# Routing statistics on ScalarE, scatters ahead of weight fetches, and layer 1's first scores ahead of the last tile's projections, in a two-layer AdaLN kernel

## The chip, the cores and the metric

The kernel runs on one core of a Trainium2 chip, as one program that computes both layers. The metric is the device time of one execution in microseconds (us). All arithmetic is in float32. Engines are named as in the profile: PE (TensorE, matrix products and transposes), PEld (its weight loads), DVE (VectorE), ACT (ScalarE), POOL (GpSimd, which also issues the indirect DMAs) and SP (SyncE, which here only issues DMAs). Each engine works through its own instructions in a fixed order.

## The reference

Eight sequences of 512 tokens, 256 values a token. Each layer is an attention part and an expert part; each part normalises the token, scales and shifts it by values made from a conditioning vector, and adds its result times a gate to the token. Layer 0's attention is a recurrence with a 16 x 16 state per head; its experts are chosen by argmax, one of eight for each token. Layer 1's attention is causal softmax attention with a table of relative biases; its experts are all computed and mixed by thresholded softmax weights.

```python
# layer 0, attention: q, k, v = silu(x @ W); q, k of unit length; beta = sigmoid(x @ Wbeta)
def step(M, inp):
    q_t, k_t, v_t, b_t = inp
    out_t = jnp.einsum('bnh,bnhd->bnd', q_t, M)
    retrieved = jnp.einsum('bnhd,bnd->bnh', M, k_t)
    delta = v_t - retrieved
    M = M + b_t[..., None, None] * jnp.einsum('bnh,bnd->bnhd', k_t, delta)
    return (M, out_t)
...
# layer 0, experts: one of 8 per token
top_idx = jnp.argmax(gate_logits, axis=-1)
for e in range(8):
    h = relu(x @ w1[e] + b1[e]);  out = out + (top_idx == e) * (h @ w2[e] + b2[e])
...
# layer 1, experts: weights below 0.1 are dropped, the rest are scaled to sum 1
for e in range(8):
    out = out + weights[:, e:e + 1] * (x @ expert_w[e] + expert_b[e])
```

## The kernel before

**Tiles.** A tile is 128 positions of each of the eight sequences; there are four (`NT`), `i` counts them and `b` the sequences. Numbers from L1 on are lines of this kernel.

**Layer 0** runs one `scan` per tile: 128 steps of the recurrence, each four DVE instructions (L741 multiply, L745 reduce, L751 multiply, L756 subtract). The side work of the scan is a list of *pieces*, each with a place, which is a scan step. `run` puts a piece into the program when the scan reaches its place, and it may not be scheduled ahead of that step's instruction; apart from that the order on each engine is the scheduler's. During the scan of tile i there are three kinds of side work:

- `front(i+1)`: statistics, normalisation and projections of the next tile's tokens. Its sums are made on ACT (L498 the sum, L504 the squares, L509 the root); DVE takes the root's reciprocal at L525.
- `follow(i-1)`: what comes after the recurrence for the tile before. `attend` makes the tokens' outputs (root mean square by ACT L919, DVE L934) and adds them to the tokens, then its `stats` take mean and variance of the outgoing tokens for the routing (DVE L950, L951, then the root on ACT, L126, and DVE L132). `route` normalises (L1013), transposes (L1018), makes the gate's logits (L1036, L1051), finds the expert and then a *slot* number for every token (L1114): tokens are sorted by expert into 15 slots of 128 rows. `experts` writes the tokens to their slots in DRAM by eight indirect DMAs (`scatter`, L1130), and works through the slots: `turn` loads a slot's rows (SP issues it) and transposes them (L1169, L1173), `fetch` gets the slot's weights by an indirect DMA of POOL (L1149, two parts, two buffers each), the slot's first half is the first product (L1192) and its activation (L1201), its second half the second product (L1211), whose result goes back to DRAM (L1216 to L1218).
- gathers of finished results and their addition to the tokens in DRAM (L1265, L1266).

Pieces of `experts` are steps of one generator, taken by `on`. The first slots of a tile are done in the same scan (places from 70), slots `late` to 14 in the next scan's list `rest`. Slots 12 to 14 of tile 2 are worked during `follow(3)`, which has no scan beside it and runs after scan 3. A piece `behind("ranks")` may not be scheduled ahead of the routing's last product on PE (L1083), `behind("attention")` not ahead of the attention part's end.

**Layer 1** starts with `prologue`, which normalises (L120 to L183) and projects (L240, L257) the tokens of sequence 0, for tiles 0 to 2 and then for tile 3, whose tokens arrive last. Then a loop over steps `n`: `scores` (L1433 PE, L1442 DVE adds the bias and takes the least, L1447 ACT's exponential), `turn` (L1459 transposes, copied by L1466 and L1468), `weigh` (L1480), and for the sequence before, `tail`, with the expert part: `weights_T` (L1590 transposes the mixing weights, L1592 copies them) and `experts` (L1598 multiplies them with the eight bias rows, L1600 copies that out, L1604 the experts' products, L1609 their weighted sum). All PSUM tiles come from `bank()`, which goes around the 7 banks of layer 0 and the 8 of layer 1.

Of the kernel before, what the change touches and what calls it, by code (L numbers as in the profile page):

```python
# [19 lines left out]
P = 128  # L20
# [43 lines left out]
def tile_two_layers(ctx: ExitStack, tc: tile.TileContext, t: dict, out: bass.AP):  # L64
# [157 lines left out]
    def prologue(b, got, xs, parts=(tuple(range(NT)),)):  # L222
# [13 lines left out]
        def values(i):  # L236
# [7 lines left out]
            w1["ready"] = nc.vector.tensor_add(  # L244
# [3 lines left out]
            ).ins  # L248
# [29 lines left out]
    with ExitStack() as l0:  # L278
# [485 lines left out]
        def attend(i, qk, V, x1, norms):  # L764
# [180 lines left out]
            def stats(b):  # L945
                h = b // 4
                if b % 4 == 0:
                    got["mv", h] = fp.tile([P, 4, 2], F32, tag="mvf", name=f"mvf{i}_{h}")
                st = fp.tile([P, 6], F32, tag="stf", name=f"stf{i}_{b}", bufs=4)
                nc.vector.bn_stats(st, x1[b])  # L950
                nc.vector.bn_aggr(got["mv", h][:, b % 4, :], st)  # L951
                if b % 4 == 3:
                    norms.append((got["mv", h], deviation(fp, "f", got["mv", h])))
# [12 lines left out]
            for h in range(2):  # L966
                pieces.append((16 * h + 25, lambda h=h: roots(h)))
                for b in range(4 * h, 4 * h + 4):
                    pieces.append((13 * h + 25 + b, lambda b=b: rest(b)))
                    pieces.append((12 * h + 30 + b, lambda b=b: stats(b)))  # L970
            return got, pieces

        def route(i, h, norms):
# [31 lines left out]
            for half in range(2):  # L1005
                rs, off = scale_offset(fp, "f", *norms[half])
# [76 lines left out]
            issued["ranks"] = nc.tensor.matmul(  # L1083
# [3 lines left out]
            ).ins  # L1087
# [51 lines left out]
        def experts(i, slot, idx, scatter):  # L1139
# [37 lines left out]
            for j, part in ((0, 0), (0, 1), (1, 0)):  # L1177
                fetch(j, part)
            with tc.issue_after(issued["fetch"]):
                scatter()  # L1180
            yield
            turn(0)
            for j in range(NSLOT):
# [21 lines left out]
                fetch(j + 1, 1)  # L1205
                yield
# [12 lines left out]
                fetch(j + 2, 0)  # L1219
# [16 lines left out]
            if i == NT - 1:  # L1236
                rows = [w1["rows"][:, b * D : (b + 1) * D] for b in range(B)]
                for b in range(B):
                    gather(b, rows[b])
                nc.vector.tensor_mul(rows[0], rows[0], gates[1][:, 0, :])  # L1240
                nc.vector.tensor_add(w1["xs"][:, i, :], rows[0], x_last)
                yield
                with tc.issue_after(w1["ready"]):
                    for b in range(1, B):
                        nc.vector.tensor_mul(rows[b], rows[b], gates[1][:, b, :])
                        nc.gpsimd.dma_start(x2d[b][i], rows[b], accum_op=ALU.add)
# [22 lines left out]
        def follow(i, qk, V):  # L1269
# [20 lines left out]
            def behind(what):  # L1290
                with tc.issue_after(issued[what]):
                    on()

            pieces += [(34, begin), (42, more), (51, more), (57, more), (60, more), (62, settle)]
# [4 lines left out]
                NT - 1: (0, 4, [10 * j for j in range(NSLOT)]),  # L1299
                NT - 2: (12, 4.3, [43, 61, 61.4]),  # L1300
            }.get(i, (11, 4.6, [8, 22, 40, 61]))
            rest = []
            for j in range(NSLOT):
                for half in range(2):
# [3 lines left out]
                    place = starts[j - late]  # L1308
                    if i == NT - 1:
                        rest.append((place + 3 * half, on))  # L1310
                    elif place < 43:
                        rest.append((place + 3 * half, on))
                    else:
                        what = "ranks" if place > 60 else "attention"
                        rest.append((place + 0.2 * half, lambda what=what: behind(what)))
# [8 lines left out]
        def load1():  # L1324
# [16 lines left out]
            put("eb", [NE, D], t["expert_b"])  # L1341
# [67 lines left out]
        for k, piece in enumerate(begun):  # L1409
            place = 102 + 4 * k if k < NT + 2 else 145 + k if k < NT + 4 else 201 + k  # L1410
            last.append((place, piece))
# [6 lines left out]
    with ExitStack() as l1:  # L1418
# [3 lines left out]
        gw, gbias, eb, ew = (w1[key] for key in ("gw", "gbias", "eb", "ew"))  # L1422

        def scores(b, c, i):
# [12 lines left out]
            for r in range(4):  # L1437
# [4 lines left out]
                nc.vector.tensor_tensor_reduce(  # L1442
# [6 lines left out]
            return made.ins  # L1449
# [40 lines left out]
        def tail(b, got):  # L1490
# [6 lines left out]
            wt = lp.tile([P, NT, NE], F32, tag="wtd", name=f"wtd{b}")  # L1497

            ys, yTt, stats, wTs = {}, {}, {}, []
# [62 lines left out]
            def weights():  # L1562
# [14 lines left out]
                nc.vector.scalar_tensor_tensor(  # L1577
# [197 lines left out]
```

## Time and profile before

| | us |
|---|---|
| median of 3 runs | 2201.99 (2200.83 to 2203.8) |
| the profiled execution | 2209.05 |
| its span | 2207.3 |
| scan 0, 1, 2, 3 (first L741 to last L756) | 244.8, 259.1, 264.4, 249.5 |
| last scan's end to the slot numbers of tile 3 | 1077 to 1166 |
| experts of tile 3, first to last product | 1199 to 1336 |
| layer 1, first scores to the end | 1353 to 2207 |

The span is the part of the execution that the profile covers; the rest of the profiled execution's time lies around it. Busy time over the whole span: PE 1730.0, DVE 1582.4, ACT 1080.0, POOL 640.6 us. In a row of a timeline the bracket at the end gives how long the engine had been idle before the instruction and what ended that.

### The profile page before, as it was taken

To read this page: it belongs to the slowest core of one execution; us is meant where nothing else is said; L and a number is where in the kernel's file an instruction comes from. 1 tells how busy PE (TensorE), PEld (TensorE's weight loads), DVE (VectorE), ACT (ScalarE), POOL (GpSimd) and SP (SyncE) were. 2 spreads that over 40 slices of the span, in tenths; PEclk is the share of its full clock that TensorE was granted. 3 is DMA by queue.
4 is the path that set the end of the run, shared out by engine and by line. 5 is a ranking of instruction groups with operands and counts; after the bars stand their busy time and mean duration, and the time that the engine had idled before them with its cause. 6 is when DMAs were issued, how large, how long until landed. Compare 5 with 4: busy or idle time off the path is not lost. (4 is left out here: it accounts for less than half of the span.)

```text
span 2207.3 us, 32493 instructions
## 1 busy us (share of the span) xinstructions
PE 1730.0 (78%) x10906; PEld 1208.3 (55%) x10906; DVE 1582.4 (72%) x4523; ACT 1080.0 (49%) x2674; POOL 640.6 (29%) x920
## 2 busy tenths in 40 slices
PE   5342047479885898649886798999999999999988
PEld 4221035269673786549765785555555555555544
DVE  5999999979989799899751004677676666666654
ACT  5253035554466545414341236785657474756421
POOL 1313013355353554524463643011110101010210
PEclk8676577689887999869997998999999999999998
DMA  5110000358104580139863873000101000010101
GB/s 165 49 50 5 0 1 11 103 181 321 50 18 138 188 325 36 49 119 335 190 124 138 288 236 71 1 20 11 27 11 25 13 22 15 20 20 6 23 17 12
DMA packets 88630, 189.58 MB, mean 86 GB/s; under 512 B 13688, under 2 KB 67104, under 8 KB 75664
## 3 DMA queue, kind: packets, MB, share of 16 engines
q0 software_dynamic: 33696, 137.43, 19.5%
q1 hardware_dynamic: 54768, 50.09, 7.9%
q8 instruction: 86, 1.41, 0.3%
q14 instruction: 80, 0.66, 0.1%
HBM read 175.10 MB, written 36.93 MB: 96 GB/s over the span
## 5 line engine op out<-in xcount | busy, mean ns | idle before, releaser
L1447 ACT ACTIVATE pr<-sc,low 128x384 f32<-128x384 f32 (+3 forms) x512 | 255.7, 556 | 197.2 <-DVE low L1442 193.8
L1442 DVE CUSTOM_DVE_ANT_0 sc<-ps,strips 128x384 f32<-128x384 f32 (+3 forms) x512 | 225.8, 486 | 87.1 <-PE ps L1433 56.3
L1192 PE MATMUL ps<-hTs,w 128*128 128x128 f32 x1920 | 243.8, 289 | 12.6 <-DMA w<-in_wrows,idx 7.8
L1192 PEld LDWEIGHTS ps<-hTs,w 128*128 128x128 f32 x1920 | 239.4, 204 | 19.9 <-issue 10.9
L745 DVE TENSOR_REDUCE state<-terms 128x16 f32<-128x272 f32 x512 | 227.3, 444 | 15.5
L1211 PE MATMUL ps<-w,act 128*128 128x256 f32 x960 | 226.4, 391 | 11.5 <-DMA w<-in_wrows,idx 8.9
L756 DVE TENSOR_TENSOR state<-state,upd 128x256 f32<-128x256 f32 x511 | 222.7, 436 | 15.0
L1604 PE MATMUL ps<-ew,hTd 128*128 128x512 f32 x512 | 232.6, 608 | 0.0
L741 DVE TENSOR_TENSOR terms<-state,K 128x256 f32<-128x256 f32 x512 | 216.2, 422 | 14.8
L751 DVE TENSOR_TENSOR upd<-K,state 128x256 f32<-128x256 f32 x511 | 214.4, 420 | 16.0
L1201 ACT ACTIVATE act<-ps,w 128x128 f32<-128x128 f32 x480 | 136.6, 372 | 148.2 <-PE ps L1192 139.5
L1211 PEld LDWEIGHTS ps<-w,act 128*128 128x128 f32 x960 | 183.8, 197 | 37.9 <-issue 7.6
L1459 PE MATMUL ps<-cst,pr 128*128 128x128 f32 x1280 | 191.7, 295 | 14.5 <-DVE low L1442 11.6
L1609 DVE SCALAR_TENSOR_TENSOR accd<-ps,wtd,accd 128x256 f32<-128x256 f32 x256 | 123.8, 483 | 100.9 <-PE ps L1604 86.4
L1459 PEld LDWEIGHTS ps<-cst,pr 128*128 128x128 f32 x1280 | 149.6, 149 | 83.6 <-DVE low L1442 24.0
L1613 POOL TENSOR_TENSOR accd<-accd,bc_g 128x256 f32<-128x256 f32 x28 | 20.3, 726 | 547.0 <-DVE accd L1609 547.0
L1149 POOL DMA_INDIRECT w<-in_wrows,idx x120 | 124.3, 1036 | 186.8 <-ACT hTs L1173 78.3
L1604 PEld LDWEIGHTS ps<-ew,hTd 128*128 128x128 f32 x512 | 96.4, 193 | 120.4 <-issue 106.6
L1433 PE MATMUL ps<-kT,qTc 32*128 32x128 f32 (+3 forms) x1024 | 132.3, 491 | 4.4 <-DVE low L1442 2.7
L1468 DVE COPY prT<-ps 128x512 f32<-128x512 f32 (+3 forms) x256 | 117.1, 484 | 10.3 <-PE ps L1459 10.0
L1466 ACT COPY prT<-ps 128x512 f32<-128x512 f32 (+3 forms) x256 | 98.6, 413 | 7.9 <-PE ps L1459 7.5
L1480 PE MATMUL ps<-prT,v 128*32 128x512 f32 (+3 forms) x1024 | 96.6, 448 | 0.0
(296 smaller groups left out, 2890.7 us busy)
## 6 DMA issues: line engine op xcount, KB each, us to landing
hs<-zero SPq DMA_DIRECT2D x4, 1920.0 KB
hslot<-hs SPq DMA_DIRECT2D x60, 128.0 KB
ys<-ysb POOLq DMA_DIRECT2D x60, 128.0 KB
x<-in_x SPq DMA_DIRECT2D x32, 128.0 KB
strips<-strip_d SPq DMA_DIRECT2D x16, 256.0 KB
out<-accd POOLq DMA_DIRECT2D x32, 128.0 KB
wm<-in_wmod SPq DMA_DIRECT2D x4, 768.0 KB
xt<-in_x SPq DMA_DIRECT2D x12, 256.0 KB
```

The lines of the kernel that those rows point to most:

```text
L741: nc.vector.tensor_mul(term[:, :, :HD], M, K[:, s, :].unsqueeze(1).to_broadcast([P, HD, HD]))
L745: nc.vector.tensor_reduce(delta, term, AX.X, ALU.add)
L751: nc.vector.tensor_mul(upd, K[:, s, :].unsqueeze(2).to_broadcast([P, HD, HD]), delta.unsqueeze(1).to_broadcast([P, HD, HD]),)
L756: yield nc.vector.tensor_sub(M, M, upd).ins
L1192: nc.tensor.matmul(ph[:, q * P : (q + 1) * P], w[:, k * FF + f * P : k * FF + (f + 1) * P], hT[:, k, :], start=(k == 0), stop=(k == 1),)
L1201: nc.scalar.activation(act[:, f, :], ph[:, q * P : (q + 1) * P], AF.Relu, bias=w[:, 2 * FF + f : 2 * FF + f + 1],)
L1211: nc.tensor.matmul(py[:, :D], act[:, f, :], w[:, f * D : (f + 1) * D], start=(f == 0), stop=(f == NFC - 1),)
L1433: made = nc.tensor.matmul(pscs[r][:, :W], qT[rows, g, o, i * P : (i + 1) * P], kT[rows, g, :W], start=True, stop=True,)
L1442: nc.vector.tensor_tensor_reduce(out=sc[:, :W], in0=pscs[r][:, :W], in1=strips[:, n, S - W :], scale=1.0, scalar=3.0e38, op0=ALU.add, op1= ...
L1447: nc.scalar.activation(pr, sc[:, :W], AF.Exp, bias=low, scale=-1.0)
L1459: nc.tensor.transpose(pt[:, (i - j) * P : (i - j + 1) * P], prs[r, i][:, j * P : (j + 1) * P], ident,)
L1604: nc.tensor.matmul(pe, hT[0][:, k, cols], ew[:, k, e : e + 2, :], start=(k == 0), stop=(k == 1),)
```

## The change

Six edits go together.

1. `stats` of tiles 0 to 2 no longer use DVE: two ACT passes per token (a copy whose accumulator gives the sum, a square that gives the sum of squared deviations, both written to a PSUM bank that nothing reads), a small multiplication per pair of tokens, and one root per four. They stand three places later. In `route` the reciprocal and offset are made from that root on DVE.
2. The routing's pieces for those tiles are moved from places 34, 42, 51, 57, 60 to 38, 45, 54, 58, 60.
3. `experts` scatters first; the first three weight fetches come behind the scatters, in two more pieces at 62.3 and 62.6.
4. The last late slots are placed at 62.1 to 62.7, behind the scatters' place, without the tie to the ranks: for tile 2 the second half of slot 12, and slots 13 and 14. The first weights of slot 14 are fetched half a slot earlier.
5. For the last tile, the multiplication and addition of sequence 0's rows, and the multiplications for the seven others, are on GpSimd instead of DVE. Tile 3's part of layer 1's prologue is a piece at step 2 of layer 1's loop; in the first eight steps what follows `scores` may not be scheduled ahead of its last DVE instruction.
6. In layer 1, the mixing weights of the four tiles lie 32 columns apart, so that one 128 x 128 transpose puts them into four groups of rows; the bias rows are loaded four times, and the four products with them are issued together by `weights_T`, each into a bank of its own and copied by ACT.

```diff
@@ -241,11 +241,11 @@
     )
-   w1["ready"] = nc.vector.tensor_add(
+   nc.vector.tensor_add(
     v[:, i, :, :HD],
...
     bv.rearrange("p (n d) -> p n d", d=HD),
-   ).ins
+   )
@@ -946,11 +946,34 @@
      got["mv", h] = fp.tile([P, 4, 2], F32, tag="mvf", name=f"mvf{i}_{h}")
-    st = fp.tile([P, 6], F32, tag="stf", name=f"stf{i}_{b}", bufs=4)
-    nc.vector.bn_stats(st, x1[b])
-    nc.vector.bn_aggr(got["mv", h][:, b % 4, :], st)
-    if b % 4 == 3:
-     norms.append((got["mv", h], deviation(fp, "f", got["mv", h])))
+    mv = got["mv", h]
+    if i == NT - 1:
+     st = fp.tile([P, 6], F32, tag="stf", name=f"stf{i}_{b}", bufs=4)
+     nc.vector.bn_stats(st, x1[b])
+     nc.vector.bn_aggr(mv[:, b % 4, :], st)
+     if b % 4 == 3:
+      norms.append((mv, deviation(fp, "f", mv)))
+    elif b % 2:
+     less = bank()
+     pair = slice(b % 4 - 1, b % 4 + 1)
+     for k in (b - 1, b):
+      nc.scalar.activation(
+       less[:, (k % 2) * D : (k % 2 + 1) * D], x1[k], AF.Copy,
+       accum_out=mv[:, k % 4, 0:1],
+      )
+     nc.scalar.mul(mv[:, pair, 0], mv[:, pair, 0], -1.0 / D)
+     for k in (b - 1, b):
+      nc.scalar.activation(
+       less[:, (k % 2) * D : (k % 2 + 1) * D], x1[k], AF.Square,
+       bias=mv[:, k % 4, 0:1], accum_out=mv[:, k % 4, 1:2],
+      )
+     if b % 4 == 3:
+      sd = fp.tile([P, 4], F32, tag="sdf", name=f"sdf{i}_{h}")
+      nc.scalar.activation(
+       sd, mv[:, :, 1], AF.Sqrt, bias=ln_eps, scale=1.0 / D
+      )
+      norms.append((mv, sd))
@@ -967,7 +990,8 @@
      pieces.append((13 * h + 25 + b, lambda b=b: rest(b)))
-     pieces.append((12 * h + 30 + b, lambda b=b: stats(b)))
+     wait = 3 if i < NT - 1 else 0
+     pieces.append((12 * h + 30 + b + wait, lambda b=b: stats(b)))
    return got, pieces
@@ -1003,7 +1027,16 @@
    for half in range(2):
-    rs, off = scale_offset(fp, "f", *norms[half])
+    if i == NT - 1:
+     rs, off = scale_offset(fp, "f", *norms[half])
+    else:
+     mv, sd = norms[half]
+     rs, off = (
+      fp.tile([P, 4], F32, tag=f"{tag}f", name=f"{tag}f{i}_{half}")
+      for tag in ("rs", "off")
+     )
+     nc.vector.reciprocal(rs, sd)
+     nc.vector.tensor_mul(off, mv[:, :, 0], rs)
     pl = bank()
@@ -1080,11 +1113,11 @@
    )
-   issued["ranks"] = nc.tensor.matmul(
+   nc.tensor.matmul(
     pr[:, B * NE : B * NE + NE], count,
...
     start=True, stop=True,
-   ).ins
+   )
    yield
@@ -1174,10 +1207,13 @@
-   for j, part in ((0, 0), (0, 1), (1, 0)):
-    fetch(j, part)
-   with tc.issue_after(issued["fetch"]):
-    scatter()
+   scatter()
+   yield
+   with tc.issue_after(issued["scatter"]):
+    fetch(0, 0)
+   yield
+   fetch(0, 1)
+   fetch(1, 0)
    yield
@@ -1203,6 +1239,8 @@
     fetch(j + 1, 1)
+    if j == NSLOT - 3:
+     fetch(j + 2, 0)
     yield
@@ -1216,7 +1254,8 @@
     nc.gpsimd.dma_start(ys_d[i][j * P : (j + 1) * P, :], ysb)
-    fetch(j + 2, 0)
+    if j != NSLOT - 3:
+     fetch(j + 2, 0)
     if i == NT - 1 and j == NSLOT // 2:
@@ -1235,15 +1274,16 @@
     rows = [w1["rows"][:, b * D : (b + 1) * D] for b in range(B)]
-    for b in range(B):
+    for b in range(3):
      gather(b, rows[b])
-    nc.vector.tensor_mul(rows[0], rows[0], gates[1][:, 0, :])
-    nc.vector.tensor_add(w1["xs"][:, i, :], rows[0], x_last)
+    nc.gpsimd.tensor_mul(rows[0], rows[0], gates[1][:, 0, :])
+    nc.gpsimd.tensor_add(w1["xs"][:, i, :], rows[0], x_last)
+    for b in range(3, B):
+     gather(b, rows[b])
     yield
-    with tc.issue_after(w1["ready"]):
-     for b in range(1, B):
-      nc.vector.tensor_mul(rows[b], rows[b], gates[1][:, b, :])
-      nc.gpsimd.dma_start(x2d[b][i], rows[b], accum_op=ALU.add)
+    for b in range(1, B):
+     nc.gpsimd.tensor_mul(rows[b], rows[b], gates[1][:, b, :])
+     nc.gpsimd.dma_start(x2d[b][i], rows[b], accum_op=ALU.add)
     yield
@@ -1287,32 +1327,35 @@
-   def behind(what):
-    with tc.issue_after(issued[what]):
+   def behind():
+    with tc.issue_after(issued["attention"]):
      on()
...
-   pieces += [(34, begin), (42, more), (51, more), (57, more), (60, more), (62, settle)]
+   if i == NT - 1:
+    routing = (34, 42, 51, 57, 60)
+   else:
+    routing = (38, 45, 54, 58, 60)
+   pieces += zip(routing, (begin, more, more, more, more))
+   pieces.append((62, settle))
...
    late, pace, starts = {
-    NT - 1: (0, 4, [10 * j for j in range(NSLOT)]),
-    NT - 2: (12, 4.3, [43, 61, 61.4]),
-   }.get(i, (11, 4.6, [8, 22, 40, 61]))
+    NT - 1: (0, 4, [(10 * j, 10 * j + 3) for j in range(NSLOT)]),
+    NT - 2: (12, 4.3, [(43, 62.1), (62.2, 62.4), (62.5, 62.7)]),
+   }.get(i, (11, 4.6, [(8, 11), (22, 25), (40, 43), (62.2, 62.7)]))
+   pieces += [(62.3, on), (62.6, on)]
    rest = []
...
       continue
-     place = starts[j - late]
-     if i == NT - 1:
-      rest.append((place + 3 * half, on))
-     elif place < 43:
-      rest.append((place + 3 * half, on))
+     place = starts[j - late][half]
+     if place == 43 and half == 0:
+      rest.append((place, behind))
      else:
-      what = "ranks" if place > 60 else "attention"
-      rest.append((place + 0.2 * half, lambda what=what: behind(what)))
+      rest.append((place, on))
    if i == NT - 1:
@@ -1338,7 +1381,10 @@
    put("gbias", [P, NE], t["gate_b1"].partition_broadcast(P))
-   put("eb", [NE, D], t["expert_b"])
+   w1["eb"] = wp1.tile([P, D], F32, name="eb1")
+   for i in range(NT):
+    nc.sync.dma_start(w1["eb"][32 * i : 32 * i + NE, :], t["expert_b"])
@@ -1407,8 +1453,8 @@
   for k, piece in enumerate(begun):
-   place = 102 + 4 * k if k < NT + 2 else 145 + k if k < NT + 4 else 201 + k
-   last.append((place, piece))
+   if k < NT + 4:
+    last.append((102 + 4 * k if k < NT + 2 else 145 + k, piece))
   run(last)
@@ -1420,6 +1466,11 @@
   gw, gbias, eb, ew = (w1[key] for key in ("gw", "gbias", "eb", "ew"))
+  wts = []
+  for k in range(2):
+   wts.append(lp.tile([P, NT, 32], F32, name=f"wtd{k}", bufs=1))
+   nc.gpsimd.memset(wts[k], 0.0)
@@ -1439,14 +1490,14 @@
     low = lp.tile([P, 1], F32, tag="low", name=f"low{b}_{i}_{n}", bufs=8)
-    nc.vector.tensor_tensor_reduce(
+    least = nc.vector.tensor_tensor_reduce(
      out=sc[:, :W], in0=pscs[r][:, :W], in1=strips[:, n, S - W :],
...
     prs[r, i] = pr
-   return made.ins
+   return made.ins, least.ins
@@ -1494,9 +1545,9 @@
    lg = lp.tile([P, NT, NE], F32, tag="lgd", name=f"lgd{b}")
-   wt = lp.tile([P, NT, NE], F32, tag="wtd", name=f"wtd{b}")
-   ys, yTt, stats, wTs = {}, {}, {}, []
+   wt = wts[b % 2][:, :, :NE]
+   ys, yTt, stats, accs = {}, {}, {}, []
@@ -1574,10 +1625,7 @@
     nc.vector.tensor_mul(lg, lg, wide(tot))
-    nc.vector.scalar_tensor_tensor(
-     wt.rearrange("p i e -> p (i e)"), lg.rearrange("p i e -> p (i e)"), 0.1,
-     lg.rearrange("p i e -> p (i e)"), ALU.is_ge, ALU.mult,
-    )
+    nc.vector.scalar_tensor_tensor(wt, lg, 0.1, lg, ALU.is_ge, ALU.mult)
     ws = row4("wsd")
@@ -1585,19 +1633,27 @@
    def weights_T():
     pt = bank()
+    nc.tensor.transpose(
+     pt[:, :P], wts[b % 2].rearrange("p i e -> p (i e)"), ident
+    )
+    wT = lp.tile([P, P], F32, tag="wT", name=f"wT{b}", bufs=1)
+    nc.vector.tensor_copy(wT, pt[:, :P])
+    pbs = [bank() for _ in range(NT)]
     for i in range(NT):
-     nc.tensor.transpose(pt[:NE, i * P : (i + 1) * P], wt[:, i, :], ident)
-    wT = lp.tile([NE, S], F32, tag="wT", name=f"wT{b}", bufs=1)
-    nc.vector.tensor_copy(wT, pt[:NE, :])
-    wTs.append(wT)
+     rows = slice(32 * i, 32 * i + NE)
+     nc.tensor.matmul(
+      pbs[i][:, :D], wT[rows, :], eb[rows, :], start=True, stop=True
+     )
+    for i in range(NT):
+     acc = lp.tile([P, D], F32, tag="accd", name=f"accd{b}_{i}", bufs=4)
+     nc.scalar.copy(acc, pbs[i][:, :D])
+     accs.append(acc)
...
     cols = slice(i * P, (i + 1) * P)
-    pb = bank()
-    nc.tensor.matmul(pb[:, :D], wTs[0][:, cols], eb, start=True, stop=True)
-    acc = lp.tile([P, D], F32, tag="accd", name=f"accd{b}_{i}")
-    nc.scalar.copy(acc, pb[:, :D])
+    acc = accs[i]
     for e in range(0, NE, 2):
@@ -1632,7 +1688,9 @@
   STEP = 4 * NT
-  side, turned = [], None
+  side = [(2 + k / 8, piece) for k, piece in enumerate(begun[NT + 4 :])]
+  turned = None
   for n in range(B * STEP + NT + 1):
@@ -1650,7 +1708,7 @@
    if n < B * STEP:
-    step = scores(b, m // NT, m % NT)
+    step, least = scores(b, m // NT, m % NT)
    if n == 0:
@@ -1658,7 +1716,11 @@
       )
-   with tc.issue_after(step):
+   with ExitStack() as order:
+    order.enter_context(tc.issue_after(step))
+    if n < 2 * NT:
+     order.enter_context(tc.issue_after(least))
     last, turned = turned, None
...
      b, m = divmod(n - NT, STEP)
```

## The prediction

> **What bounds the kernel now.** I first cut the execution by stage: time, busy microseconds of each engine, granted clock.
>
> ```profile
> core 0: us, PE busy (x) PEld busy (x) DVE busy (x) ACT busy (x) POOL busy (x), PEclk, DMA share, GB/s
> 562.00:826.40 264.40, 217.27 (x1522) 181.89 (x1521) 234.77 (x597) 149.04 (x407) 129.42 (x196) 0.88 0.39 139
> 1163.40:1199.40 36.00, 16.92 (x100) 15.34 (x100) 6.35 (x18) 5.94 (x20) 14.54 (x16) 0.74 0.46 168
> 1199.40:1335.80 136.40, 121.16 (x767) 111.34 (x768) 3.34 (x11) 47.09 (x158) 67.04 (x78) 0.94 0.69 225
> 1400.00:2000.00 600.00, 587.11 (x3526) 324.84 (x3524) 409.45 (x1440) 379.56 (x837) 66.88 (x88) 0.98 0.08 18
> ```
>
> Scan 2 (first row) is DVE's: 235 of 264 us busy, and the rest of DVE's time is waiting. Layer 1 (last row) is PE's, 587 of 600. The second row is neither: 36 us in which no engine is busy for half the time. So a DVE instruction saved counts in a scan, PE time counts in layer 1, and in that hole the chain of waits counts. Next, the waits inside the scans, from DVE's and then POOL's timeline (start, duration, idle before in brackets):
>
> ```profile
> 383.62 0.18 DVE L934 RECIPROCAL ms<-ms 128x4 f32<-128x4 f32 x1 [2.05 <-ACT ms L919]
> 470.26 0.17 DVE L525 RECIPROCAL rsa<-sda 128x2 f32<-128x2 f32 x1 [10.49 <-ACT sda L509]
> ...
> 430.76 1.00 POOL L1149 DMA_INDIRECT w<-in_wrows,idx  x1 [0.30 <-issue]
> 432.06 1.03 POOL L1130 DMA_INDIRECT hs<-x,slot  x1 [0.31 <-issue]
> 442.34 0.97 POOL L1130 DMA_INDIRECT hs<-x,slot  x1 [2.84 <-DMA w<-in_wrows,idx]
> 445.78 0.97 POOL L1130 DMA_INDIRECT hs<-x,slot  x1 [2.48 <-DMA w<-in_wrows,idx]
> ```
>
> The 10.49 us begin on POOL. Three weight fetches (428.03 to 431.8) stand ahead of eight scatters, and the last two scatters wait for fetches that are still under way. The slots' first rows come back only at 454.1; ScalarE idles 11.36 us until then (hTs L1173, 454.83), and the root L509 that DVE needs is 15.1 us behind it in ScalarE's order. Scan 2 has the same with 8.57 us. Then the hole, from PE's, DVE's and POOL's timelines:
>
> ```profile
> 1148.15 0.69 PE L1169 MATMUL ps<-cst,hslot 128*128 128x128 f32 x2 [5.11 <-DMA hslot<-hs]
> 1154.45 0.60 PE L1018 MATMUL ps<-cst,xnf 128*128 128x128 f32 x4
> 1198.28 0.69 PE L1169 MATMUL ps<-cst,hslot 128*128 128x128 f32 x2 [18.65 <-DMA hslot<-hs]
> ...
> 1165.49 0.17 DVE L1114 CAST slot<-slotf 128x8 uint32<-128x8 f32 x1
> ...
> 1181.05 1.03 POOL L1130 DMA_INDIRECT hs<-h_last,slot  x1 [0.17 <-issue]
> 1190.62 0.96 POOL L1130 DMA_INDIRECT hs<-h_last,slot  x1 [0.30 <-issue]
> ```
>
> Tile 3's routing (from L1018) could begin when its input is ready, at 1147.35, but PE first waits for tile 2's slot 13 (5.11 us) and multiplies the second half of slot 12. Its slot numbers are ready at 1165.66; the scatters start at 1181.05, because three weight fetches, the last at 1178.23 behind ScalarE's work on slot 14, precede them.
>
> **The change, part by part.**
>
> *Statistics (tiles 0 to 2, in scans 1 to 3).*
>
> ```profile
> L950 DVE BATCH_NORM_STATS2 stf<-x x32: 386/416/421, 359.3 to 1145.4; 128x6 f32<-128x256 f32 x32
> L951 DVE BATCH_NORM_AGGREGATE mvf<-stf x32: 154/171/183, 360.0 to 1145.8; 128x2 f32<-128x6 f32 x32
> ```
>
> Removed per scan: 8 x (0.416 + 0.171) = 4.7 us of DVE. Side work fills the 29 ns by which each recurrence instruction waits for the one before it (14.8 us over 512 in the page); 16 such gaps reopen, 0.5 us. Net 4.2, three times. Added to ScalarE: the same sums in `front` take 0.388 + 0.196 (L498, its read) and 0.484 + 0.202 (L504, its read), 1.27 a token, with the small multiplications some 11 us per scan. ScalarE is busy 138 of 259, 149 of 264 and 98 of 250 us, so they lie beside DVE, except where DVE waits for ScalarE in order: at L934, at the reciprocal that now follows the sums' root, and at the logits (L1051). The routing pieces move 3 to 4 scan steps (1.91 us each), the logits' piece only 3 steps behind the statistics' end for half 0, that is 5.7 us, while the chain from L132 to the logits took 8.1 us in scan 1 and 9.4 in scan 2. So a wait of 2.4 to 3.7 is new there; I take 2.8 in scans 2 and 3, where DVE also meets L934 and L132 two steps apart, and 0.4 to 1.0 for each of the others. Of the present L934 stalls (2.05, 4.12, 2.31) the first should go, the others become about 2.9. Sums without the scatter: scan 1 -4.2 - 2.05 + 1.9 = -4.3; scan 2 -4.2 - 1.2 + 3.7 = -1.7; scan 3 -4.2 + 0.6 + 3.2 = -0.4.
>
> *Scatter ahead of the fetches (scans).* Three fetch issues of about 1.3 and the waits 2.84 and 2.48 are 9.2 us, and the slots' rows no longer queue behind weights in the transfers: I take 10.5 in scan 1. The root, 469.94 now, then comes at 459.4; L525 stands two scan steps earlier in DVE's order (79 for 81), so DVE passes step 81 at 459.4 + 2 x 1.91 = 463.2 instead of 470.4: -7.2, which is 3 beyond the statistics. The same 3 in scan 2; nothing in scan 3, where PE runs some 8 us ahead of DVE's need. Scans: -7.3 - 4.7 - 0.4 = -12.4, between -28 (both L525 stalls gone entirely) and +3. Slot 0's weights now come after the scatters, by about 10 us; the first slots have no one waiting on them in a scan.
>
> *The hole.* Slot 12's second half is moved behind the routing, so L1018 starts at 1147.4: -7.1, and the slot numbers are ready near 1158.6. The scatters start there, 8 x 1.27 end at 1168.8. What is late next: fetch (14,1), now behind them on POOL, lands 6 to 9 us after its issue (the spans seen later in this tile: 1233.16 to 1239.33, 1259.27 to 1266.93), near 1177, and slot 14's second half takes 3.6. Tile 3's slot 0 then starts near 1181 instead of 1199.43: -18. Its weights are requested only 10 us ahead instead of 29, and today's prefetch hides about 2 of what slots 0 to 2 would wait, so I take -16, between -8 and -20.
>
> *First scores ahead of tile 3's projections.* PE's gap of 4.94 us before L179 (1345.94) is filled with 12 scores. Against this, ScalarE now runs tile 3's normalisation behind 12 exponentials (0.556 each) and changes tables twice more at 1.28 us, and GpSimd's multiply and add on row 0 (0.72 each, its L1217 row) wait behind five gathers instead of DVE's 0.42. I take -0.5, between -3 and +4. The Trainium skill ("ScalarE: Activation LUTs", What ACT_TABLE_LOAD costs) counts 1.28 for a load plus 1.38 for the drain, 2.66 for every change of set; by it this term would be 2.8 worse, +2.3. The trace's first exponential starts 20 ns behind its load (1352.78 + 1.28, then 1354.08).
>
> *Layer 1's weights.* Per batch the bias took four matmuls:
>
> ```profile
> L1598 PE MATMUL ps<-eb,wT x64: 374/478/791, 1517.6 to 2193.6; 8*128 8x256 f32 x64
> ```
>
> 0.43 each after each other; in four row groups they should run at once (the scores' four groups start 10 ns apart), saving 3 x 0.43, and one transpose for four at 0.11 saves 0.3. Against it PE now waits for DVE's copy (0.27 for 128 columns, by L1076, and the way there and back, 0.65 together) and for four free banks (up to 0.45), with all PE work queued behind. -0.4 to -0.9 per batch, eight times: -4.5, between -7 and +3.
>
> Sum: -12.4 - 16 - 0.5 - 4.5 = -33. The execution of the profile took 2209.05 us (span 2207.3), 7 over the median 2201.99; 2209.05 - 33 is 2176 there, and 2169 as a median.
>
> **The rivals.**
>
> 1. *ScalarE becomes late in the scans*: 11 us more of it, in pairs of sums that nothing interrupts, stand ahead of the roots and activations. For it: L934 and L525 wait for ScalarE already. Against: it idles 100 us per scan. Then the scans give nothing: -21, 2181.
> 2. *The hole's gain is half given back*: tile 3's slots draw 225 GB/s and POOL is busy half of the time, so slots started earlier wait for weights; -8 there, -25 in all, 2177.
> 3. *Slower: the four banks of bias.* weights_T now takes five of eight PSUM banks in turn, and four come free only when ScalarE's copies are reached, behind exponentials. PE is the bound there. Ten exponentials at 0.556 are 5.6 us per batch, 45 in all instead of -4.5: 2202 - 28.5 + 45 = 2218. It decides from 4.2 us of wait per batch (28.5 + 4.4, over 8). Against: ScalarE is busy 380 of 600 us and mostly waits for DVE.
> 4. *The change doesn't do what it says*: something that the trace of before can't show holds tile 3's scatters or their rows where they are, and the bias matmuls follow each other as now. Then the statistics' -6.4 and some +1.5 of new waits remain, -5: 2197, about no change.
>
> **How the numbers follow.** The forecast has 0.52, rival 1 0.18, rival 2 0.13, rival 3 0.10, rival 4 0.07. 0.2% (4.4 us) is about what a measurement can tell from no change. Faster by more: 0.83 (forecast and rivals 1 and 2); same 0.06, from rival 4; slower 0.11, rival 3 and a little of 4. Range: below, all terms at their good ends but the scans at about -25: 2202 - 25 - 18 - 3 - 6 = 2150; above, rivals 1 and 2 together with the start at +4 and layer 1 at +2, 2202 + 0 - 8 + 4 + 2 = 2200, and 2196 leaves out about the chance of rivals 3 and 4.
>
> **What would show it.** Right: DVE busy some 4.7 us less per scan; L525's stalls of 10.49 and 8.57 shrink to under 7 and 5; scatters at 1158 (less what the scans gave) directly behind the slot numbers, with slot 0 of tile 3 about 18 us earlier beside the stage before it; L1598's quartets 10 ns apart. Wrong: DVE idle behind ScalarE at the new reciprocal or the logits over 4 us per scan; PE's idle time before L1169 of tile 3 still above 10 us; PE waiting for ScalarE's accd copies in layer 1.

## The result and the profile after

The changed kernel takes 2189.0 us (median of 17 runs, 2171.38 to 2200.82) against 2203.8 (17 runs, 2190.41 to 2211.5) beside it: ratio 0.9932, interval 0.9907 to 0.9957, some 15 us faster. Faster was right; 33 us was more than twice too much, though 2189 lies between 2150 and 2196. The profiled executions differ by 13.8 us (2209.05 and 2195.24, spans 2207.3 and 2193.5), so the parts can be read from them. In the changed kernel's numbering the logits are L1084, the slot numbers L1147, scatter L1163, fetch L1182, slot products L1228 and L1249, row multiplications L1285, scores L1484 and L1493, exponentials L1498, transposes of probabilities L1510, bias products L1646.

| part of the span | before | after | change | forecast |
|---|---|---|---|---|
| scans 1 to 3 (end of scan 0 to end of scan 3) | 777.2 | 771.3 | -5.9 | -12.4 |
| end of scan 3 to tile 3's last expert product | 258.5 | 246.4 | -12.1 | -16 |
| from there to the first batch's mixing weights (DVE's copy of them) | 175.6 | 200.7 | +25.1 | -0.5 |
| from there to the end of the last instruction | 692.2 | 671.5 | -20.7 | -4.5 |

The scan times ahead of the prediction begin at each scan's first subtraction (L756), 1.4 us behind its first L741, so they add up to less. Two small errors and two large ones of opposite sign. Of the 25.1, 19.8 stand ahead of the first transposed probabilities; the way from those to the weights took 152.5 us before and 157.9 after, and kernels with the changed kernel's code there (e1, e4, e6, e11 and itself) spread from 151.6 to 157.9, so the rest is not put down to the change. The changed kernel by stage:

```profile
558.20:820.40 262.20, 219.07 (x1522) 182.00 (x1521) 231.88 (x582) 157.18 (x444) 130.00 (x196) 0.90 0.41 146
1162.60:1182.10 19.50, 18.02 (x114) 16.30 (x112) 4.28 (x8) 6.21 (x21) 14.96 (x17) 0.97 0.41 145
1317.60:1360.50 42.90, 15.80 (x79) 10.28 (x79) 6.33 (x32) 16.87 (x33) 22.03 (x28) 0.64 0.43 86
1400.00:2000.00 600.00, 583.84 (x3561) 327.90 (x3563) 411.40 (x1457) 386.33 (x852) 66.94 (x88) 0.97 0.08 17
```

The columns are those of the prediction, and the first row is scan 2 again. DVE is busy 231.9 us in it instead of 234.8; in scan 1 it is 231.1 instead of 231.2 and in scan 3 226.0 instead of 229.7, where the prediction's sign was 4.7 less in each. The old hole is closed: 19.5 us between slot numbers and slot 0, PE busy 18. A new one stands in the third row: 42.9 us from the last expert product to the first transposed probabilities (23.1 before), with every engine idle for about half of it or more.

*Scan and old hole*, from DVE's, PE's and POOL's timelines:

```profile
416.42 0.19 DVE L1084 TENSOR_TENSOR lg<-ps,gbias 128x32 f32<-128x32 f32 x1 [3.33 <-PE ps L1069]
461.54 0.17 DVE L525 RECIPROCAL rsa<-sda 128x2 f32<-128x2 f32 x1 [3.67 <-ACT sda L509]
...
1162.45 0.17 DVE L1147 CAST slot<-slotf 128x8 uint32<-128x8 f32 x1
...
1149.21 0.93 PE L1051 MATMUL ps<-cst,xnf 128*128 128x128 f32 x4 [3.35 <-ACT xnf L1046]
...
1162.90 1.05 POOL L1163 DMA_INDIRECT hs<-h_last,slot  x1 [14.50 <-DVE idx L1157]
```

L525's 10.49 us shrank to 3.67 (scan 2's 8.57 to 5.6 in two parts) and L934 no longer waits, but 3.33 us at the logits are new. The scatters start 0.3 us behind the slot numbers, as forecast. The routing's products, though, waited not for slot 13's rows but for their own input, and began 78.0 us after the scan instead of 77.1.

*The new hole*, from PE's, ACT's, POOL's and DVE's timelines:

```profile
1323.42 0.94 PE L1484 MATMUL ps<-kT,qTc 32*128 32x128 f32 x16 [0.67 <-ACT kT L261]
1344.30 2.28 PE L1484 MATMUL ps<-kT,qTc 32*128 32x384 f32 x8 [19.94 <-DVE low L1493]
1351.86 0.69 PE L179 MATMUL ps<-cst,xnc 128*128 128x128 f32 x2 [5.28 <-ACT xnc L172]
1360.46 0.52 PE L1510 MATMUL ps<-cst,pr 128*128 128x128 f32 x3 [0.60 <-issue]
...
1344.28 4.90 ACT L1498 ACTIVATE pr<-sc,low 128x128 f32<-128x128 f32 x12 [8.05 <-DVE low L1493]
1349.19 1.28 ACT L126 ACT_TABLE_LOAD   x1
...
1342.30 1.61 POOL L1285 TENSOR_TENSOR rows<-rows,gate 128x256 f32<-128x256 f32 x1
...
1343.94 0.29 DVE L1493 CUSTOM_DVE_ANT_0 sc<-ps,strips 128x128 f32<-128x128 f32 x1 [43.84 <-POOL rows L1285]
```

The first scores are on PE at 1323.4, 29 us earlier than before, and then PE stands for 19.94 us: DVE's first score instruction waits until 1343.94 for GpSimd's last row multiplication. GpSimd reaches it after eight gathers, eight other operations and six DMA issues, one after another from 1321.93. Only then come twelve exponentials, and behind them ScalarE's table load and the root of tile 3's normalisation, and its projections.

### The profile page after: what moved, and what is told of

Read it like the earlier page. It is cut to its first block, busy times and chain, and to the rows that moved or that the text cites. A ratio compares the mean times of both kernels' runs of the same rounds, so it can differ in the third digit from the quotient of the medians.

```text
span 2193.5 us, 32582 instructions
## 1 busy us (share of the span) xinstructions
PE 1724.0 (79%) x10882; PEld 1211.0 (55%) x10882; DVE 1567.5 (71%) x4466; ACT 1105.2 (50%) x2784; POOL 647.9 (30%) x931
## 3 DMA queue, kind: packets, MB, share of 16 engines
q0 software_dynamic: 33696, 137.43, 19.5%
## 5 line engine op out<-in xcount | busy, mean ns | idle before, releaser
L1498 ACT ACTIVATE pr<-sc,low 128x384 f32<-128x384 f32 (+3 forms) x512 | 255.5, 556 | 193.5 <-DVE low L1493 190.1
L1493 DVE CUSTOM_DVE_ANT_0 sc<-ps,strips 128x384 f32<-128x384 f32 (+3 forms) x512 | 225.5, 485 | 142.5 <-PE ps L1484 69.5
L1228 PE MATMUL ps<-hTs,w 128*128 128x128 f32 x1920 | 246.7, 291 | 22.5 <-DMA w<-in_wrows,idx 17.3
L1228 PEld LDWEIGHTS ps<-hTs,w 128*128 128x128 f32 x1920 | 241.9, 207 | 31.7 <-issue 19.5
L1249 PE MATMUL ps<-w,act 128*128 128x256 f32 x960 | 225.7, 390 | 11.0 <-DMA w<-in_wrows,idx 8.9
L756 DVE TENSOR_TENSOR state<-state,upd 128x256 f32<-128x256 f32 x511 | 222.2, 435 | 15.0
L741 DVE TENSOR_TENSOR terms<-state,K 128x256 f32<-128x256 f32 x512 | 216.8, 423 | 16.0
L1237 ACT ACTIVATE act<-ps,w 128x128 f32<-128x128 f32 x480 | 136.6, 371 | 151.6 <-PE ps L1228 150.6
L1249 PEld LDWEIGHTS ps<-w,act 128*128 128x128 f32 x960 | 183.5, 196 | 37.0 <-ACT hTs L1206 6.2
L1510 PE MATMUL ps<-cst,pr 128*128 128x128 f32 x1280 | 191.6, 294 | 14.3 <-DVE low L1493 10.9
L1510 PEld LDWEIGHTS ps<-cst,pr 128*128 128x128 f32 x1280 | 148.6, 148 | 84.6 <-DVE low L1493 23.9
L1660 PEld LDWEIGHTS ps<-ew,hTd 128*128 128x128 f32 x512 | 97.1, 194 | 113.4 <-issue 101.1
L1484 PE MATMUL ps<-kT,qTc 32*128 32x128 f32 (+3 forms) x1024 | 133.7, 490 | 25.2 <-DVE low L1493 22.6
L1182 POOL DMA_INDIRECT w<-in_wrows,idx x120 | 124.1, 1034 | 86.4 <-ACT hTs L1206 24.5
L1484 PEld LDWEIGHTS ps<-kT,qTc 32*128 32x128 f32 x1024 | 59.4, 189 | 78.6 <-DVE low L1493 31.9
```

The costliest lines, as they stand in the source:

```text
L741: nc.vector.tensor_mul(term[:, :, :HD], M, K[:, s, :].unsqueeze(1).to_broadcast([P, HD, HD]))
L756: yield nc.vector.tensor_sub(M, M, upd).ins
L1228: nc.tensor.matmul(ph[:, q * P : (q + 1) * P], w[:, k * FF + f * P : k * FF + (f + 1) * P], hT[:, k, :], start=(k == 0), stop=(k == 1),)
L1237: nc.scalar.activation(act[:, f, :], ph[:, q * P : (q + 1) * P], AF.Relu, bias=w[:, 2 * FF + f : 2 * FF + f + 1],)
L1249: nc.tensor.matmul(py[:, :D], act[:, f, :], w[:, f * D : (f + 1) * D], start=(f == 0), stop=(f == NFC - 1),)
L1484: made = nc.tensor.matmul(pscs[r][:, :W], qT[rows, g, o, i * P : (i + 1) * P], kT[rows, g, :W], start=True, stop=True,)
```

## The experiments

**e1: the seven row multiplications back on DVE.**

```diff
-  nc.gpsimd.tensor_mul(rows[b], rows[b], gates[1][:, b, :])
+  nc.vector.tensor_mul(rows[b], rows[b], gates[1][:, b, :])
```

> The changed kernel, with only the seven multiplications of the last tile's rows put back on DVE. Theory A (the layer-1 pool lies on memory that layer 0 gives back, so the first score instruction on DVE waits for the last multiplication on GpSimd, which stands at the end of a 22 us chain of gathers, multiplications and DMA issues there): the first DVE instruction of the scores moves from 1343.9 to about 1334 of the span and the first transpose of the probabilities from 1360.5 to about 1351, 10 us off the total. Theory B (something else holds the scores, and the multiplication is only the last to be named): both stay within 2 us.

Ratio to the kernel before 0.9906 (0.9874 to 0.9938). The scores on DVE open at 1335.7, right behind the last multiplication, and the first transposes come at 1352.3: theory A. The runs are only 4 to 6 us faster than the changed kernel's, not 10, and the two intervals overlap. From its DVE timeline:

```profile
1335.04 0.42 DVE L1285 TENSOR_TENSOR rows<-rows,gate 128x256 f32<-128x256 f32 x1 [0.87 <-DMA rows<-ys,slot]
1335.70 0.29 DVE L1493 CUSTOM_DVE_ANT_0 sc<-ps,strips 128x128 f32<-128x128 f32 x1 [0.24 <-DVE rows L1285]
```

**e2: tile 3's projections ahead of the scores again.**

```diff
-  if k < NT + 4: last.append((102 + 4 * k if k < NT + 2 else 145 + k, piece))
+  place = 102 + 4 * k if k < NT + 2 else 145 + k if k < NT + 4 else 201 + k
+  last.append((place, piece))
...
-  side = [(2 + k / 8, piece) for k, piece in enumerate(begun[NT + 4 :])]
+  side = []
...
-  if n < 2 * NT: order.enter_context(tc.issue_after(least))
```

> The changed kernel, with tile 3's part of the prologue put back ahead of layer 1's loop and without the tie of the first steps to the scores' DVE instructions. Theory A: the multiplications still open the scores at about 1344, but tile 3's projections are then done, so the first transpose of the probabilities comes at about 1350 instead of 1360.5: 10 us off. Theory B (scores ahead of the projections cost nothing, the loss is all in the wait for GpSimd): the first transpose stays at 1360 or later, no gain.

Ratio 0.9879 (0.9843 to 0.9915). DVE's scores still open at 1343.3, on GpSimd's last multiplication, and the first transposes come at 1351.4, 9 us earlier than in the changed kernel: theory A. The runs are some 11 us faster. So there are two losses of 8 to 9 us, one from each half of edit 5.

```profile
1343.30 0.29 DVE L1493 CUSTOM_DVE_ANT_0 sc<-ps,strips 128x128 f32<-128x128 f32 x1 [7.42 <-POOL rows L1285]
1351.39 2.98 PE L1510 MATMUL ps<-cst,pr 128*128 128x128 f32 x12
```

**e3: both undone, all row operations on DVE.** (e1 and e2 together; row 0's two operations on DVE too, the others behind tile 3's values as in the kernel before.)

> The changed kernel, with both undone: all nine operations on the last tile's rows back on DVE, tile 3's projections ahead of the scores. Theory A: from the last expert product to the first transpose of the probabilities 23 us as in the kernel before (42.9 in the changed one), 20 off the changed kernel's time, about 35 below the kernel before. Theory B (the hole's gain is lost in layer 1 whatever stands at its start, because transfers or the clock are late): 10 off or less.

2172.85 against 2203.45, ratio 0.9857 (0.9826 to 0.9888). The first transposes come 23.3 us behind the last expert product, the weights 174.9: the kernel before's 23.1 and 175.6. That is theory A. By the trace the start cost the changed kernel some 20 us, by the runs 16, and all the rest of the change is worth about 31.

**e4: statistics of tiles 0 to 2 back on DVE**, at the new places.

```diff
-  if i == NT - 1:   # both in stats and in route
+  if True:
```

> The changed kernel, with the statistics of tiles 0 to 2 back on DVE (batch-norm instructions), at the changed kernel's places. Theory A (side instructions on DVE hide part of the recurrence's own waits and starts, so that the eight pairs are worth about 1.4 us a scan, not 4.2, and the waits at the logits take that back): scans 1 to 3 together within 4 us of the changed kernel's 778. Theory B (the pairs cost their full 4.7 us a scan and the waits at the logits stay): scans 12 to 14 us longer.

Ratio 0.998 (0.9961 to 0.9999), about 0.5% lost; scans 1 to 3 take 781.3 us. The four kernels with the changed kernel's scans and statistics (it, e1, e2, e3) take 771.1 to 773.8. Nine us: theory A, as I had put it, fell. (The 778 of the expectation does not stand; by the measure of the table the changed kernel's scans are 771.3.) L934's waits are back, 3.70 and 2.06 us; e7 gives the rest.

**e7: the kernel before, each of those batch-norm pairs issued twice.**

```diff
   nc.vector.bn_aggr(got["mv", h][:, b % 4, :], st)
+  if i < NT - 1:
+      nc.vector.bn_stats(st, x1[b])
+      nc.vector.bn_aggr(got["mv", h][:, b % 4, :], st)
```

> The kernel before, with the two batch-norm instructions of tiles 0 to 2 issued twice per token. It measures their worth on DVE by themselves: by their durations 4.7 us a scan, scans 1 to 3 together 14 us longer. By theory A (an independent instruction between two dependent ones hides part of the second's start) about 1.5 us a scan, 4 to 5 in all; waits for ScalarE can take some of either.

Ratio 1.0023 (1.0001 to 1.0045). I split DVE's time in scan 1 by the trace, an instruction counting only from where the one before it ends:

| scan 1, us | recurrence | side work | gaps under 0.25 | longer waits |
|---|---|---|---|---|
| before | 213.7 | 18.8 | 15.2 | 12.9 |
| e7, pairs twice | 212.7 | 22.6 | 14.7 | 10.2 |
| e4, pairs once | 213.9 | 19.7 | 15.5 | 10.5 |
| after, none | 215.0 | 17.3 | 16.0 | 8.7 |

Eight more pairs are 4.7 us by their durations and 3.3 without their overlaps (the rest of the side work's 3.8 is a copy, L739, that overlaps less); the recurrence's own instructions, which then overlap the pairs, lose 1.0, the gaps 0.4. Net 1.9, and the same split gives 1.8 and 1.9 in scans 2 and 3. In scans 1 and 2 the waits shrink by more than that, so the scans themselves are no longer: 772.6 us for all three, where kernels with the pairs once show 777.2 and 771.1 (before, e5). The 1.9 is near theory A's 1.5; it rests on the split, not on a longer scan. With e4, where it gives 1.4 to 1.7: 1.4 to 1.9 a scan by themselves, and L934's waits for the rest.

**e5: layer 1's weights alone, on the kernel before.** (Edit 6 of the change.)

> The kernel before, with only layer 1's mixing weights and bias products changed. Theory A (the four bias products take 2.5 us of PE a batch one after another and 0.7 side by side, the transposes 0.27 less, and the expert product behind them starts without a break of 0.6, so a batch is 2.6 us shorter less a wait of 0.35): from the first batch's weights to the end 692 becomes about 672, 20 us off the total. Theory B (layer 1's gain in the changed kernel comes from what its start left done earlier): less than 8 us off.

Ratio 0.9927 (0.9901 to 0.9954), 2183.35 against 2200.08. From the first weights to the end 677.1 us instead of 692.2: theory A, at three quarters of its size. Alone it brings as much as the whole change. PE's row for the bias products in the changed kernel (L1646), as the one shown of before, then a quartet in its timeline, then from the kernel before's timeline one bias product and sixteen products of as many columns in layer 0:

```profile
L1646 PE MATMUL ps<-eb,wT x64: 373/426/479, 1518.7 to 2159.1; 8*128 8x256 f32 x64
...
1518.66 0.71 PE L1646 MATMUL ps<-eb,wT 8*128 8x256 f32 x8 [0.38 <-DVE wT L1642]
...
1517.62 0.69 PE L1598 MATMUL ps<-eb,wT 8*128 8x256 f32 x2
...
1168.98 3.62 PE L1211 MATMUL ps<-w,act 128*128 128x256 f32 x16
```

The two records of a product last 478 and 374 ns in both kernels; what differs is their overlap: a quartet's first four records start 7 ns apart. A record counted only from where the one before it ends, the eight records (two for each product) occupied PE for 2.50 us a batch and now 0.71. The expert products behind them take 27.7 instead of 28.3, the transposes 0.26 instead of 0.53, and PE's new wait for DVE's copy is 0.38: together 2.3 a batch, 18 for eight. Issuing the four together would not do it without the row groups: sixteen records of 256 columns one after another take 3.62 us (L1211), so eight would take about 1.8.

**e6: fetches ahead of the scatters again, for all tiles.**

```diff
+  for j, part in ((0, 0), (0, 1), (1, 0)): fetch(j, part)
+  with tc.issue_after(issued["fetch"]): scatter()
-  scatter()
...
-  with tc.issue_after(issued["scatter"]): fetch(0, 0)
...
-  fetch(0, 1); fetch(1, 0)
```

> The changed kernel, with the first three weight fetches ahead of the scatters again. Theory A (the order on GpSimd's queue makes the hole: the third fetch waits for a buffer that slot 14 frees): tile 3's scatters start at about 1177 instead of 1163, its slot 0 at about 1195 instead of 1182, and scan 1's wait at L525 returns to some 10 us: 15 to 20 us more in all. Theory B (the late slots' places alone made the gain): scatters within 4 us of the changed kernel's.

Ratio 1.0021 (1.0 to 1.0041). L525 in scan 1 waits 8.7 us again (3.7), scans 1 to 3 take 775.7. Tile 3's scatters start 18.1 us behind the slot numbers instead of 0.3 (at 1176.0), its slot 0 at 1191.0: theory A there. But the slot numbers come 81.6 us after the scan instead of 91.2, and the last expert product 247.2 instead of 246.4. So in this pair the stage as a whole gained nothing. From the slot numbers to the last product, scattering first for tile 3 is worth some 10 us in every kernel: 151.6 to 160.5 with it, 165.4 to 170.2 without. Whether it is also what makes the slot numbers late is not shown; they spread by 8 us among kernels with the same order (84.9 to 93.0). Ahead of that the two differ in scan 3: in e6 tile 2's first product starts 99.5 us before the scan's end and its twelfth slot ends 6.5 before it; in the changed kernel the one is at -101.1 and the other at +6.0, because its slots wait for weights 11.3 us in all (8.8 at L1228, 2.5 at L1249) instead of 3.4. The runs put e6 some 0.9% above the changed kernel, its profiled span only 3 us: the changed kernel's profiled execution is 6 us above its median, e6's 3 below, and what makes that spread was not seen.

**e9: as e3, fetches first for tile 2 alone.** (e6's lines under `if i == NT - 2`.)

> e3 (the changed kernel with layer 1's start as before), with the first weight fetches ahead of the scatters for tile 2 alone. In the changed kernel's scan 3 the fetches of tile 2's slots stand behind the addition of the slot before on GpSimd's queue; its slots begin at 101 us before the scan's end and the twelfth ends 6 to 10 after it, where e6 needs from -99.5 to -6.5. Theory A (with the scatters ahead the scheduler puts the queue in that order, so weights come late and the attention and routing of tile 3 start late): slot numbers of tile 3 at about 82 us after the scan instead of 87 to 93, scatters still at once behind them, the expert stage 5 to 8 us earlier than e3's 245 after the scan, about 6 off the total. Theory B (the late routing is a matter of the run, its spread is 85 to 93): no change.

2169.02, ratio 0.9837 (0.9804 to 0.987). GpSimd's queue in scan 3, first the changed kernel, then e9:

```profile
986.59 0.72 POOL L1255 TENSOR_TENSOR ysb<-ysb,w 128x256 f32<-128x256 f32 x1 [3.39 <-ACT ysb L1254]
987.46 1.01 POOL L1182 DMA_INDIRECT w<-in_wrows,idx  x1 [0.15 <-issue]
988.48 0.59 POOL L1256 DMA_DIRECT2D ys<-ysb  x1
989.37 1.05 POOL L1182 DMA_INDIRECT w<-in_wrows,idx  x1 [0.30 <-issue]
```

```profile
987.58 1.05 POOL L1182 DMA_INDIRECT w<-in_wrows,idx  x1 [0.30 <-issue]
990.13 1.00 POOL L1182 DMA_INDIRECT w<-in_wrows,idx  x1 [1.50 <-ACT hTs L1206]
992.89 0.72 POOL L1263 TENSOR_TENSOR ysb<-ysb,w 128x256 f32<-128x256 f32 x1 [1.77 <-ACT ysb L1262]
```

GpSimd adds a bias to each slot's result, and waits for ScalarE before it does. In the changed kernel the fetch of the first weights of the slot after next stands behind that addition (987.46 behind 986.59); in e9 it is ahead of it (990.13 ahead of 992.89). The fetch of the second part is behind it in both. The twelfth slot ends 5.7 us before the scan's end. That half of theory A holds. The routing gained little: slot numbers at 86.0, where kernels with the changed order show 84.9 to 93.0, and the total is within e3's interval. The last expert product comes 240.9 us after the scan, 4.2 ahead of e3's, but 245.6 in e10, which has the same lines for tile 2. So the late weights do not settle when tile 3's routing starts; what does stays open.

**e10: fetches first for tiles 1 and 2.**

> As e9, with the fetches ahead for tiles 1 and 2. It tells what scattering first is worth in scan 2: by theory A of the prediction (the root's wait at L525) scan 2 gets 3 to 5 us longer than e3's 267, by the other (fetches and scatters share the queue, the order gives nothing there) it stays within 2.

2166.13, ratio 0.9826 (0.9785 to 0.9866), the lowest median of all. Scan 2 takes 263.9 us (e3 266.9): there scattering first gives nothing.

**e11: tile 2's late slots at their old places.**

```diff
-  NT - 2: (12, 4.3, [(43, 62.1), (62.2, 62.4), (62.5, 62.7)]),
+  NT - 2: (12, 4.3, [(43, 43.2), (61, 61.2), (61.4, 61.6)]),
```

> The changed kernel, with tile 2's late slots at their old places (second half of slot 12 at 43.2, slots 13 and 14 at 61 and 61.4), scatters first. Theory A (the second half of slot 12 and slot 13's rows hold up the routing's products on PE): tile 3's slot numbers 5 to 7 us later than the changed kernel's 91 after the scan. Theory B (the routing's inputs come late anyway, so PE's order there costs nothing): within 2 us.

Ratio 0.9974 (0.9945 to 1.0003). Slot numbers at 95.3 us after the scan, 4 behind the changed kernel's and outside the 84.9 to 93.0 of the kernels with the new places: nearer theory A, by one profile. But the last expert product comes at 247.1, where those show 242.8 to 248.4. The 4 us are given back in the slots.

**e8: as e3, the logits' pieces later.**

```diff
-  routing = (38, 45, 54, 58, 60)
+  routing = (38, 48, 54, 60, 61)
```

> The changed kernel with the start of layer 1 as before (e3), and the routing's pieces of tiles 0 to 2 at 38, 48, 54, 60, 61 instead of 38, 45, 54, 58, 60. Theory A (DVE waits at the logits because their pieces stand too close behind the chain on ScalarE and PE): the waits of 3.3, 2.5 + 3.6, 2.8 + 1.4 us at the logits nearly go, scans 1 to 3 some 8 to 12 us shorter than e3's 774. Theory B (the routing's end is what the scan needs, and a later slot number is given back at the first slots and L525): no change within 3 us.

Ratio 0.9877 (0.985 to 0.9905). The waits at the logits go but for 0.75 us, and in scans 1 and 2 come back two steps later, at the copy of the counts (L1109: 4.4 and 4.7 us, 1.0 in e3): theory B there. Scan 3, which prepares no further tile, is 3.6 shorter.

## Why the prediction was right or wrong

- **Layer 1's start failed, and it is why the gain was less than half.** The step said "I take -0.5, between -3 and +4"; it was 20 to the first transposes. I priced GpSimd's multiply and add on row 0 and left out the seven other multiplications that the same edit moves. Nothing in the arithmetic ties the scores to those rows; but layer 1's tiles lie in memory that layer 0's pools give back, the gates that the multiplications read among it, and the program makes the first DVE instruction there wait for GpSimd. In the compiled program that instruction waits for the count that the last multiplication makes on GpSimd, although the tile that it writes shares no byte with the gates: the new pool as a whole waits for the old ones. In the changed kernel, e1 and e2 it started within 0.3 us of the last multiplication, on whichever engine that was (in e1 DVE's own order is enough for that). The profile before hinted at it: the seven multiplications stood right ahead of the first scores on DVE. The second half, ScalarE's exponentials ahead of tile 3's root, I had set off against a PE gap of 4.94 us; it cost 8.5 (e2) to 11.5 (e1 against e3, 34.9 and 23.3 us; e3 also moves row 0's two operations back). Row 0's own result, which I had priced by the two durations, came 8.7 us behind the start of the first gather instead of 3.7 (e3); in these runs that lay beside the other two losses. The table load itself took 1.28 us and the root started 20 ns behind it (1350.49), so the 2.66 of the Trainium skill ("ScalarE: Activation LUTs", What ACT_TABLE_LOAD costs) was not paid here either.
- **Layer 1's weights: right mechanism, size off by four.** -4.5, between -7 and +3, was -15 (e5) to -21. That this error made up for most of the start's loss is luck. The term was the bias product: 0.43 each, where PE spends 0.62 on the two records of each, and the wait, 0.65 to 1.1, was 0.38; the 0.6 that the expert products gained was not in the sum at all. The Trainium skill ("TensorE: Matmul & The Clock Gate", Part 3: Packing small matmuls) gives 3.07 times for four row groups of 32 rows and 512 columns; 2.50 to 0.71 here is 3.5 times.
- **Statistics: mis-sized, and made up for by a wait.** 4.2 a scan is 1.4 to 1.9 by itself (e4, e7). I counted the gaps that side work fills, not that the recurrence's next instruction overlaps it. The L934 waits of scans 2 and 3, which I kept at 2.9, went, worth 5.8 in e4. What they and L525 gave was taken at the logits: DVE's waits over 0.25 us add up to 31.9 us in the three scans before and 30.2 after.
- **The waits at the logits**: 2.8 and less than 1 were 3.3, 2.8 and 3.3, 2.6 and 1.4, in scan 2 over the 4 us that I had named as a sign of being wrong; e8 shows that they are mostly the queue at the routing, not its places. The scans' -12.4 is not there: the kernel before's scans take 777.2 and 771.1 us (before, e5), the changed one's 771.1 to 773.8. A single profile's scans spread by 6 us, and I summed terms smaller than that. Of the 3 us a scan for scattering first, scan 1 shows some (L525 waits 3.7 to 5.5 us in the kernels that scatter first for tile 0, 8.7 in e6), scan 2 nothing (e10).
- **The hole**: -16, between -8 and -20. Kernels with the old order show 258.5, 251.3 and 256.2 us from scan 3 to the last product (before, e5, e7), with the new one 242.8 to 248.4: about -10. Of the two terms one failed: the slot numbers were to come 7 us earlier and came 3 later behind the scan, because the routing's own input was late, not PE; why it was late stays open. The other was too small: from the slot numbers to slot 0 took 19.5 us instead of 33.8, where the forecast has 22.4. That slot 0 starts at 1182, forecast 1181, is chance: the scans had ended 6 us earlier, and from the scan's end it moved by 11, not 18. "The first slots have no one waiting on them in a scan" was the wrong sentence: in scan 3 tile 2's slots fell 13 us behind for want of weights (e6, e9), though how much of that reached tile 3 was not resolved. Undoing either of the change's two means for the hole (e6, e11) left the last product within the spread of the others, 247.2 and 247.1 us after the scan.
- Rival 3 did not happen: the profile names no wait of layer 1's PE for the copies out of the four banks. Rival 1's outcome came, scans that gave nothing clear of their spread; its reason, a late ScalarE, can at most lie behind the waits at the logits, which the profile puts down to PE, and was not taken apart further. Rival 2 did not happen: tile 3's slots took 135.5 us from first to last product, 136.4 before.

## What to carry to other kernels

Before moving instructions to an engine that is idle, look for whoever next takes the memory that these instructions read: where pools are given back, the first instruction in the new pool can wait for the last one that used the old, here GpSimd's. A step moved ahead is worth only what its followers can use; scores that stand on PE until DVE may write gain nothing, and what they put ahead of the critical normalisation on ScalarE is lost. An edit of several parts is best taken apart: here one of six brought as much as the whole (e5), and without another, edit 5, the gain doubles (e3).

## What the runs showed of the hardware

An independent instruction between two dependent ones on DVE cost far less than its duration: sixteen batch-norm instructions of 4.7 us took 1.9 us net of DVE's time in scan 1 (before and e7, by the split above). Four products with 8 rows in different row groups of PE took 0.71 us, as long as 1.1 of them did before (2.50 for four). With the fetch of a slot's first weights queued behind an addition on GpSimd instead of ahead of it, tile 2's twelve slots took 108.8 us instead of 93.5 (e3, e9; 104 to 111 in the kernels that scatter first for tile 2, 93 to 96 in those that fetch first).
